# Layer 0 of a four-layer convolution kernel: two depthwise blocks on channel groups of 32 split by row and column parity, one tap of each VectorE block as a ScalarE product added by a transfer, images kept singly

## The chip, the cores and the metric

The kernel runs on one core of a Trainium2 chip. A core has a matrix engine (TensorE, "PE" in the profile, with its weight loads as "PEld"), a vector engine (VectorE, "DVE"), an engine for pointwise functions (ScalarE, "ACT"), a general engine (GpSimd, "POOL"), an engine that only issues transfers (SyncE, "SP") and 16 DMA engines that move data. The metric is the device time of one execution in microseconds. Each engine takes its instructions strictly in its own order; semaphores tie the engines to each other.

## What is computed

The input x has 32 images of 96 channels with 56 by 56 pixels, in float32. Four layers follow each other, each of the form x + f(norm(x)), where norm is a group norm over three channels. The change touches layer 0 alone. Cut to what matters, layer 0 is

```
xn = group_norm(x)
h  = einsum('nchw,oc->nohw', xn, w_exp)          # 96 -> 576 channels
h  = silu(bn1(h))
h  = depthwise 3x3 convolution(h, w_dw)          # each channel by itself, zero padding
h  = silu(bn2(h))
s  = sigmoid(w_se2 @ silu(w_se1 @ mean(h)))      # one factor per image and channel
h  = einsum('nchw,oc->nohw', h * s, w_proj)      # 576 -> 96 channels
y  = x + (bn3(h) + xn)
```

Layers 1 to 3 (a wavelet convolution, a quantised bottleneck, a 9x9 convolution) are the same before and after the change.

## The kernel before, in words

**Blocks.** The 576 channels of layer 0 stand in blocks of 128 partitions. The depthwise convolution of blocks 0, 1 and 2 is made tap by tap on 128x3136 tiles: the first tap by ScalarE (`first_tap`, L349), the other eight by VectorE as h = pad * w + h (`tap`, L354), 24 instructions an image. Block 3 ("ab") and the half block 4 ("c") go through TensorE: `quarters` (L382) multiplies a 64x64 diagonal matrix per tap with shifted windows of a padded tile, in the four 64x64 quarters of the array, nine taps accumulated in PSUM. Float32 matmuls appear twice in the trace, as two passes, so one call of `quarters` is 36 matmuls and 72 rows of the trace. There are six calls an image (four for ab, two for c).

**Steps.** All work on an image is cut into short steps, written as a letter and numbers:

- s, u, m, q, v, w, b, n: the group norm. s and q are ScalarE sums (L281), u and v small matmuls, m, w and b small VectorE work, w with a power on GpSimd (L302). n writes the normalised image xn (ScalarE, L315), of which there is one buffer.
- e: `expand`, one matmul group of w_exp (L329) and its eviction with silu by ScalarE into a padded tile (L341). `e20` is block 2, quarter 0 of the rows.
- f, t: the taps of blocks 0 to 2. z: `end_block`, the second silu in place with its sum over the pixels (L360). a, c: the depthwise calls for ab and c with their evictions (L360).
- g: the factors per channel: totals (VectorE), two sets of small matmuls (L412, L419), a sigmoid (L426, with a load of its function table), and the scaling of w_proj (L430).
- r: ScalarE prepares the residual in place (L321). p: `project` (L441 to L443), a quarter of the rows each, 20 rows of the trace. d: VectorE adds it to the image (L449). o: channel statistics for the next layer (L90), the store of the image, the fetch of a later one.

**Order.** `L0_ORDER` is one row of such steps, run once per image; a "-" behind a step means the image before, "--" the one before that, "+" the next. `run_steps` walks the row for n = -2 to 33 and issues every step for the image it names. For TensorE, VectorE and ScalarE this written order is the order on the engine (`manual_schedule`). SyncE and GpSimd get theirs from the framework, which here follows the program's order.

**PSUM.** Steps e, a, c and p share one pool of three buffers ("mm"), given out in turn: each such step waits until the one three places earlier in the row has been read out.

**Transfers.** Images come and go in pairs. `fetch` (L215) loads two images at once into one of two tiles of 2352 KB. After the second image of a pair `store_images` writes both into six scratch tensors of 16 channels (L166, six DMAs). In these tensors the four phases of 14 columns of all images lie beside each other, so the contiguous run is 112 bytes for a pair and 56 bytes for one image; the last two images are stored singly (L166 for image 30, L153 for image 31). In between, SyncE issues transfers that build filter matrices for layers 1 and 3 (`aside`, L567 and L594), a share of them at each store, until image 27. All of these stand in one queue. A fetch waits until the tile that it overwrites has been stored.

**Start.** Image 0 is normalised first; then the filter tables of layers 1 and 3 are made, on GpSimd above all, in memory that layer 0 takes over afterwards ("late" tiles: three of the five h tiles, the ab and c tiles, the second image tile). `fetch(2)` is issued when that memory is free.

The functions that the change touches, with the line numbers of the profile:

Of the kernel before, what the change touches and what calls it, by code (L numbers as in the profile page):

```python
# [21 lines left out]
HW = H * W  # L22
# [14 lines left out]
HALO = 4  # L37
MAGIC = 12582912.0
# [23 lines left out]
    e00 e01 e02 e03 z0- f0 a3- z2- c1- e10 e11 t01 t02 g0- e12 t03 e30 e40 g1- e13 t04 g2- g3-  # L62
    e31 e32 t05 e33 g4- t06 t07 s+ f1 t11 p0- u+ m+ p1- q+ t08 d0- v+ w+ p2- t12 e41 d1- p3- d2- t13
    t14 e20 e21 d3- o- b+ t15 e42 t16 e43 e22 e23 f2 a0 t17 t21 a1 n+ t22 t18 t23 t24 t25 t26 t27 r
    z1 t28 c0 a2
# [115 lines left out]
def layer0(ctx, tc, S, x, w, y0, norm1, tables, aside):  # L181
# [16 lines left out]
    DV, AB, CC = 3, 3, 4  # L198
    ND = NBLK + 1
    COL = (0, 1, 2, 3, 5)  # L200
# [8 lines left out]
    pairs = [cp.tile([C, H * NPH, 2, W4], F32, tag="xt0", name="xt0")]  # L209

    def fetch(b):

        if b < B:
            pair = pairs[b // 2 % 2]
            nc.sync.dma_start(pair, x[b // 2])  # L215
            for j in range(2):
                xs[b + j] = pair, pair[:, :, j, :]
# [3 lines left out]
    wexp = load("l0_wexp", [C, NBLK * 128])  # L221
    mid = load("l0_mid", [128, 9, ND])
    wdw = load("l0_wdw", [128, ND, 9])
    wse1 = load("l0_wse1", [128, ND, SEH])
    wse2 = load("l0_wse2", [SEH, ND * 128])
    bse1 = load("l0_bse1", [SEH, 1])
# [4 lines left out]
    for j in range(2):  # L231
        g, b_, m, v = (mid[:, 4 * j + i, :] for i in range(4))
        r = cp.tile([128, ND], F32, tag=f"r{j}", name=f"r{j}")
        nc.gpsimd.tensor_scalar(r, v, EPS_L0, None, ALU.add)
        nc.gpsimd.tensor_tensor(r, r, S.mhalf[:, :ND], ALU.pow)
        s = cp.tile([128, ND], F32, tag=f"s{j}", name=f"s{j}")
        nc.vector.tensor_tensor(s, g, r, ALU.mult)
        o = cp.tile([128, ND], F32, tag=f"o{j}", name=f"o{j}")
        nc.vector.tensor_tensor(o, m, s, ALU.mult)
        nc.vector.tensor_tensor(o, b_, o, ALU.subtract)  # L240
        sc.append(s)
        bi.append(o)
# [8 lines left out]
    diag = cp.tile([128, 2, 9, HALF], F32, tag="diag", name="diag")  # L251
    hpad = padded(cp, nc, 3, F32, "hpad") + padded(cp, nc, 1, F32, "hhalf", HH)
# [3 lines left out]
    eye2 = h2s[1].rearrange("p h w -> p (h w)")[:, :HALF]  # L256
    nc.vector.tensor_tensor(eye2, S.ident[:, :HALF], S.ident[:, HALF:], ALU.add)
    for k in (AB, CC):
        for t in range(9):
            nc.vector.tensor_scalar(diag[:, k - AB, t, :], eye2, wdw[:, COL[k], t : t + 1], None, ALU.mult)  # L260

    ims = {}

    def image(b):

        if b not in ims:
            pair, xt = xs.pop(b)
            ims[b] = {
                "b": b, "pair": pair, "xt": xt, "h2": [None] * DV, "ps": [None] * NP,
                "pad": [hpad[(DV * b + k) % 2] for k in range(DV)] + hpad[2:],  # L270
                "ss": sm.tile([128, ND], F32, tag="ss", name="ss"),
            }
        return ims[b]
# [49 lines left out]
    def expand(im, k, i):  # L323

        c = COL[k]
        rows = slice(2 * i * RT, 2 * (i + 1) * RT)
        ps = psum.tile([128, 2, 512], F32, tag="mm", name="ps")
        for j in range(2):
            nc.tensor.matmul(  # L329
                ps[:, j, :NT], wexp[:, k * 128 : k * 128 + 128],  # L330
                im["xn"][:, j, rows, :].rearrange("c h w -> c (h w)"), start=True, stop=True,
            )

        parts = [(slice(128), 2 * i * RT, slice(2 * RT))]
        if k == CC:
            lo, up = slice(64), slice(64, 128)
            parts = [(up if i // 2 else lo, i % 2 * 2 * RT, slice(2 * RT))]
            parts += [[], [(up, -1, slice(2 * RT - 1, 2 * RT))], [(lo, HH, slice(1))], []][i]
        for p, r0, rows in parts:
            n = rows.stop - (rows.start or 0)  # L340
            nc.scalar.activation(  # L341
                window(im["pad"][k][p], p.stop - (p.start or 0), 0, 0, r0, n).rearrange("p r (w j) -> p j r w", j=2),
                ps[p, :, :NT].rearrange("p j (r w) -> p j r w", w=W2)[:, :, rows],
                AF.Silu, bias=bi[0][p, c : c + 1], scale=sc[0][p, c : c + 1],
            )
# [16 lines left out]

    def end_block(im, k):
        silu2(k, im["h2"][k], im["h2"][k], im["ss"][:, k : k + 1])
# [5 lines left out]
    def quarters(k, pad, tiles):  # L370

        ps = psum.tile([128, 2, 512], F32, tag="mm", name="psd")
        for t in range(9):
            for j in range(2):
                for r in range(2):
                    c = r ^ j
                    p = slice(r * HALF, (r + 1) * HALF)
                    at = (2 * tiles[r] * RT + t // 3) * PITCH + t % 3  # L380
                    v = pad[p, at : at + 2 * RT * PITCH].rearrange("p (r w) -> p r w", w=PITCH)
                    nc.tensor.matmul(  # L382
                        ps[c * HALF : (c + 1) * HALF, j, :NT].rearrange("p (r q m) -> p r q m", q=W4, m=2),
                        diag[p, k - AB, t, :], phases(v[:, :, :W], j), start=(t == 0), stop=(t == 8),
                    )
        return ps

    def depthwise_ab(im, i):
        if i == 0:
            im["hab"] = hab  # L390
            im["pab"] = sm.tile([128, 2, NP], F32, tag="pab", name="pab")
        ps = quarters(AB, im["pad"][AB], (i, i))
        for j in range(2):
            silu2(3 + j, im["hab"][:, i, j, :], ps[:, j, :NT], im["pab"][:, j, i : i + 1])

    def depthwise_c(im, i):

        if i == 0:
            im["hc"] = hc
            im["pc"] = sm.tile([128, 2], F32, tag="pc", name="pc")  # L400
        ps = quarters(CC, im["pad"][CC], (i, i))
        silu2(5, im["hc"][:, i], ps[:, :, :NT], im["pc"][:, i : i + 1])


    def totals(im):
        nc.vector.tensor_reduce(im["ss"][:, 3:5], im["pab"], AX.X, ALU.add)
        nc.vector.tensor_tensor(im["ss"][:, 5:6], im["pc"][:, 0:1], im["pc"][:, 1:2], ALU.add)

    def squeeze(im):
        ps = psm.tile([SEH, 1], F32, tag="sm", name="pse")  # L410
        for k in range(ND):
            nc.tensor.matmul(ps, wse1[:, k, :], im["ss"][:, k : k + 1], start=(k == 0), stop=(k == ND - 1))  # L412
        im["s1g"] = sm.tile([SEH, 1], F32, tag="s1g", name="s1g")
        nc.scalar.activation(im["s1g"], ps, AF.Silu, bias=bse1, scale=1.0 / HW)
# [7 lines left out]
    def gates(im):  # L422
        gt = im["gate"] = sm.tile([128, ND + 1], F32, tag="gate", name="gate")
        nc.vector.tensor_tensor(gt[:, :ND], im["pg"], mid[:, 8, :], ALU.add)
        nc.vector.tensor_tensor(gt[:, ND:], im["pg"][:, ND - 1 : ND], mid[:, 8, ND - 1 : ND], ALU.add)
# [7 lines left out]
    def project(im, i):  # L433
# [3 lines left out]
        for j in range(2):  # L437
            out = ps[:C, j, :NT].rearrange("c (m r q) -> c r q m", m=2, q=W4)
            hab, hc = (im[n].rearrange("p i j (r q m) -> p i j r q m", q=W4, m=2) for n in ("hab", "hc"))
            for k in range(DV):  # L440
                nc.tensor.matmul(out, wg[:, k, :], phases(im["h2"][k][:, rows], j), start=(k == 0), stop=False)  # L441
            nc.tensor.matmul(out, wg[:, 3 + j, :], hab[:, i, j], start=False, stop=False)  # L442
            nc.tensor.matmul(out, wg[:, 5 + (i // 2 ^ j), :], hc[:, i % 2, j], start=False, stop=True)  # L443
# [10 lines left out]
    def store(im):  # L454
        b = im["b"]
        channel_stats(nc, sm, im["xt"], mv_all[:, b, :], "t")
        store_images(nc, y0, im)
        if b % 2:
            fetch(b + 3)
# [10 lines left out]
        "e": expand, "f": first_tap, "t": tap, "z": end_block, "a": depthwise_ab, "c": depthwise_c,  # L470
# [11 lines left out]
    hab = late.tile([128, NP, 2, NT], F32, tag="hab", name="hab")  # L482
    wg = late.tile([128, ND + 1, C], F32, tag="wg", name="wg")
    h2s.append(late.tile([128, H, W], F32, tag="h24", name="h24"))
    hc = late.tile([128, 2, 2, NT], F32, tag="hc", name="hc")
    pairs.append(late.tile([C, H * NPH, 2, W4], F32, tag="xt1", name="xt1"))
# [836 lines left out]
def layouts(a):  # L1323
# [29 lines left out]
    def columns(names, blocks):  # L1353
        return np.stack([blocks(a[n]) for n in names], axis=1)

    i0, i2 = "L0_conv_", "L2_conv_"
# [4 lines left out]
        "l0_wexp": np.concatenate([a[i0 + "w_exp"], a[i0 + "w_exp"][512:]]).T,  # L1361
        "l0_mid": columns(
            [i0 + n for n in ("g1", "b1", "m1", "v1", "g2", "b2", "m2", "v2", "b_se2")], quartered
        ),
        "l0_wdw": quartered(a[i0 + "w_dw"].reshape(MID, 9)),
        "l0_wse1": quartered(a[i0 + "w_se1"].T),
        "l0_wse2": quartered(a[i0 + "w_se2"]).transpose(2, 1, 0).reshape(SEH, (NBLK + 1) * 128),
        "l0_bse1": a[i0 + "b_se1"].reshape(SEH, 1),
        "l0_wproj": apart(quartered(a[i0 + "w_proj"].T)),
# [44 lines left out]
```

## Time and profile before

| What | Value |
|---|---|
| Three timed runs, us | 6365.32, 6370.07, 6379.44; median 6370.07 |
| Profiled execution, span, us | 6375.2 (what lies around the span is not given) |
| Layer 0, first expand to last VectorE add | 28 to 3233 us |
| VectorE busy, 100 to 1600 us (layer 0) | 1415.85 of 1500 |
| TensorE busy, the same stretch | 1465.64 |
| ScalarE busy, the same stretch | 988.69 |
| DMA share, the same stretch | 0.23 |
| First fetch, issue to first use | 0.72 to 14.07 us |
| Fetch behind the tables, issued | 96.65 us |
| First tap of image 0, of image 31 | 41.4 us, 3091.3 us |
| End of the last tap in layer 0 | 3193 us |
| Start of the norm that closes layer 0 | 3236.8 us |

The page gives busy time by engine, by slice of the span and by group of instructions; a group names the line, the engine, the operation, its output and inputs, the number of instructions, their busy time and mean duration, and the idle time ahead of them with what ended it. Concurrent matmuls count once in "busy" and each for itself in "mean". One image of layer 0 takes about 99 us, so a sum per image and engine is the natural unit.

### The profile page before, as it was taken

The page shows a single profiled execution, that of the slowest core. Times are in us where ns is not written, and L with a number is a line of the kernel's source. Part 1 is how long each engine was busy: PE and PEld are TensorE (multiplying, and loading weights), DVE is VectorE, ACT ScalarE, POOL GpSimd, SP SyncE. Part 2 cuts the span into 40 slices and gives each one's busy share as a digit, 9 for nine tenths or more (in the row PEclk, how much of TensorE's full clock was granted, in tenths as well). Part 3 has the DMA queues.
Part 4 walks back from the last instruction along what each step waited for, and adds up shares of the span by engine and source line. Part 5 has one row for each costly group of instructions (what it writes and reads, how often), then busy time and mean ns, then how long its engine had stood idle before and what let it go on. Part 6 is the DMA issues. An engine that isn't in the chain of part 4 may idle for free.

```text
span 6375.2 us, 115759 instructions
## 1 busy us (share of the span) xinstructions
PE 6012.5 (94%) x49064; PEld 3561.4 (56%) x49064; DVE 5173.6 (81%) x5533; ACT 4051.7 (64%) x5716; POOL 236.1 (4%) x157
## 2 busy tenths in 40 slices
PE   6999999999999999999969999989999999999699
PEld 3444444444444444444445666667777777777344
DVE  8999999999999999999947666667777776776577
ACT  6667676676666766667535655567767676776355
POOL 5000000000000000000000000000000000000000
PEclk8999999999999999999979999999999999999899
DMA  3112222122221222212465866568787786863788
GB/s 96 17 38 57 50 45 35 42 55 54 41 36 36 51 54 43 42 26 37 24 90 145 152 147 146 127 29 54 42 53 41 51 44 46 48 46 27 183 249 245
DMA packets 1305764, 452.95 MB, mean 71 GB/s; under 512 B 1123150, under 2 KB 1301062, under 8 KB 1303326
## 3 DMA queue, kind: packets, MB, share of 16 engines
q1 hardware_dynamic: 1305246, 445.54, 47.3%
q8 instruction: 386, 6.32, 0.5%
q14 instruction: 132, 1.08, 0.1%
HBM read 284.44 MB, written 214.08 MB: 78 GB/s over the span
## 4 chain that ended last, share of the span: by engine, by line
PE 72%; ACT 14%; DMA 6%; DVE 4%; SPq 2%; issue 1%; POOL 1%; ACTq 0%; DVEq 0%; POOLq 0%
PE psd L382 18%; PE psd L1066 11%; PE ps L329 11%; PE pc L782 6%; PE ps L1047 6%; PE psj L441 5%; ACT junk L281 4%; PE psj L1103 3%; DVE h L354 2%; DMA raw<-tdiff 2%; ACT hi L1019 2%; DMA X<-y 2%; ACT hpad L341 2%; PE psj L442 2%; PE pc L766 2%; ACT a L1037 2%
## 5 line engine op out<-in xcount | busy, mean ns | idle before, releaser
L354 DVE SCALAR_TENSOR_TENSOR h<-hpad,l_wdw,h 128x3136 f32<-128x3136 f32 x768 | 2662.4, 3481 | 37.3 <-ACT h L349 23.5
L1066 PE MATMUL psd<-apad,diag 64*64 64x392 bf16 x20736 | 927.1, 331 | 96.3 <-ACT a L1037 51.6
L329 PE MATMUL ps<-xn,l_wexp 96*128 96x392 f32 x2560 | 893.1, 500 | 6.4 <-ACT xn L315 4.4
L1066 PEld LDWEIGHTS <-diag 64*64 64x64 bf16 x20736 | 691.3, 107 | 328.0 <-issue 151.1
L382 PE MATMUL psd<-hpad,diag 64*64 64x392 f32 x9216 | 831.1, 511 | 0.0
L341 ACT ACTIVATE hpad<-ps,o,s 128x784 f32<-128x784 f32 x512 | 545.7, 1081 | 302.5 <-PE ps L329 299.2
L329 PEld LDWEIGHTS ps<-xn,l_wexp 96*128 96x128 f32 x2560 | 478.6, 191 | 374.9 <-issue 36.5
L612 ACT COPY T<-raw 32x112 f32<-32x112 f32 (+2 forms) x1440 | 462.8, 384 | 312.2 <-DMA raw<-tdiff 229.3
L1037 ACT ACTIVATE u<-ps,o,s 128x784 int16<-128x784 f32 x576 | 536.7, 1003 | 159.8 <-PE ps L1047 140.9
L441 PE MATMUL psj<-h,wg 128*96 128x392 f32 x1536 | 603.8, 529 | 17.0 <-DVE wg L430 8.0
L1037 ACT ACTIVATE a<-psd,o,s 128x784 int16<-128x784 f32 x448 | 424.1, 998 | 305.8 <-PE psd L1066 305.7
L382 PEld LDWEIGHTS psd<-hpad,diag 64*64 64x64 f32 x9216 | 347.1, 131 | 467.6 <-issue 433.0
L1047 PE MATMUL ps<-hi,l_w1q 96*128 96x392 f32 x1280 | 461.5, 361 | 9.2 <-ACT hi L1019 9.2
L1220 PE MATMUL pc<-x,T 128*112 128x416 f32 (+1 forms) x1152 | 416.9, 524 | 52.0 <-DMA raw<-tdiff 48.1
L782 PE MATMUL pc<-x,T 128*112 128x416 f32 (+1 forms) x1152 | 445.1, 522 | 0.0
L1047 PE MATMUL ps<-lo,l_w1q 96*128 96x392 f32 x1280 | 437.2, 342 | 0.0
L382 PE MATMUL psd<-hhalf,diag 64*64 64x392 f32 x4608 | 417.6, 510 | 0.0
L441 PEld LDWEIGHTS psj<-h,wg 128*96 128x96 f32 x1536 | 247.0, 166 | 285.8 <-issue 250.7
L341 ACT ACTIVATE hhalf<-ps,o,s 64x56 f32<-64x56 f32 (+1 forms) x192 | 163.6, 852 | 342.3 <-PE ps L329 340.5
L1220 PEld LDWEIGHTS pc<-x,T 128*112 128x112 f32 x1152 | 203.7, 178 | 264.7 <-issue 236.1
L360 ACT ACTIVATE hab<-psd,o,s 128x392 f32<-128x392 f32 x256 | 170.9, 672 | 248.6 <-PE psd L382 248.6
L382 PEld LDWEIGHTS psd<-hhalf,diag 64*64 64x64 f32 x4608 | 182.7, 132 | 223.0 <-issue 223.0
(209 smaller groups left out, 7673.6 us busy)
## 6 DMA issues: line engine op xcount, KB each, us to landing
X<-y SPq DMA_DIRECT2D x192, 392.0 KB
y<-xt SPq DMA_DIRECT2D x180, 392.0 KB
xt<-in_x_dram SPq DMA_DIRECT2D x16, 2352.0 KB
y<-y SPq DMA_DIRECT2D x96, 392.0 KB
xt<-y SPq DMA_DIRECT2D x96, 392.0 KB
out_dram<-y SPq DMA_DIRECT2D x96, 392.0 KB
twav<-zwav SPq DMA_DIRECT2D x768, 36.8 KB
raw<-twav SPq DMA_DIRECT2D x96, 168.0 KB
```

Source lines behind the costliest of these rows:

```text
L281: nc.scalar.activation(junk, im["xt"][:, i * 2 * RT * NPH : (i + 1) * 2 * RT * NPH], func, bias=bias, accum_out=im[name][:, i : i + 1])
L329: nc.tensor.matmul(ps[:, j, :NT], wexp[:, k * 128 : k * 128 + 128], im["xn"][:, j, rows, :].rearrange("c h w -> c (h w)"), start=True, sto ...
L341: nc.scalar.activation(window(im["pad"][k][p], p.stop - (p.start or 0), 0, 0, r0, n).rearrange("p r (w j) -> p j r w", j=2), ps[p, :, :NT] ...
L354: nc.vector.scalar_tensor_tensor(h2, window(im["pad"][k], 128, t // 3 - 1, t % 3 - 1, 0, H), wdw[:, k, t : t + 1], h2, ALU.mult, ALU.add,)
L382: nc.tensor.matmul(ps[c * HALF : (c + 1) * HALF, j, :NT].rearrange("p (r q m) -> p r q m", q=W4, m=2), diag[p, k - AB, t, :], phases(v[:, ...
L441: nc.tensor.matmul(out, wg[:, k, :], phases(im["h2"][k][:, rows], j), start=(k == 0), stop=False)
L612: nc.scalar.copy(to.rearrange("x t (p s) -> x t p s", p=NPH), v[:, k])
L782: nc.tensor.matmul(ps[:PH, to], st["T"][j][:, h, k, :], st["x"][:, j, h, of], start=False, stop=(n == NK - 1))
L1037: nc.scalar.activation(out, ps, AF.Identity, bias=o[:, c : c + 1], scale=s[:, c : c + 1])
L1047: nc.tensor.matmul(ps[:, j, :NT], w1[:, k * 128 : k * 128 + 128], im[part][:, r0 : r0 + RT, :].rearrange("c h w -> c (h w)"), start=(part ...
L1066: nc.tensor.matmul(ps[q, j, :NT].rearrange("p (r w) -> p r w", w=W), diag[p, k, t, :], v, start=(t == 0), stop=(t == 8))
L1220: nc.tensor.matmul(ps[:, :, to], st["T"][:, h, k, :], st["x"][:, h, :, of], start=(n == 0), stop=(n == NK - 1))
```

## The change

Blocks 3 and 4 leave the padded tiles. Their 192 channels form six groups of 32. A group's expanded image is written as a "plane" of 128 partitions: four copies of the 32 channels, one for each parity of row and column, each of 28 by 28 pixels. `expand_phases` makes one plane by eight matmuls of 96x32 and one eviction. `filtered` makes the depthwise convolution for four groups (or parts) at once: a 128x32 matrix sums up to four taps in one matmul; taps that cross to a neighbouring row of planes use the lower or the upper 64 partitions. A call is 32 matmuls, six calls an image as before.

Of each VectorE block tap 8 is made by ScalarE into a tile `tmp` (there is one) and added to h by a DMA that GpSimd issues (`product`, step x). VectorE keeps seven taps.

Images are held singly in three tiles; each is stored and fetched by itself. The row of steps is another, with the image's work spread over three rows.

```
-    e00 e01 e02 e03 z0- f0 a3- z2- c1- e10 e11 t01 t02 g0- e12 t03 e30 e40 g1- e13 t04 g2- g3-
-    e31 e32 t05 e33 g4- t06 t07 s+ f1 t11 p0- u+ m+ p1- q+ t08 d0- v+ w+ p2- t12 e41 d1- p3- d2- t13
-    t14 e20 e21 d3- o- b+ t15 e42 t16 e43 e22 e23 f2 a0 t17 t21 a1 n+ t22 t18 t23 t24 t25 t26 t27 r
-    z1 t28 c0 a2
+    t05- g0-- f1- z2-- e30- t06- g1-- g2-- g3-- g4-- t07- x08- e20- e23- s t11- p3-- p1-- d3-- r- u
+    e21- t12- t13- e22- m d1-- t14- q p0-- t15- v p2-- z0- t16- w t17- x18- f2- b n d0-- d2-- a0-
+    a3- a2- e00 t21- t22- e01 t23- e02 t24- t25- e03 z1- t26- t27- a1- x28- f0 c0- c1- e10 e12 e13
+    e33 e32 o-- e11 e31 e40 t01 t02 t03 t04 e41
...
+    images = [cp.tile([C, H * NPH, W4], F32, tag="xt0", name="xt0")]
     def fetch(b):
         if b < B:
-            pair = pairs[b // 2 % 2]
-            nc.sync.dma_start(pair, x[b // 2])
+            xs[b] = images[b % 3]
+            nc.sync.dma_start(xs[b], x[b])
...
+    def expand_phases(im, g):
+        ps = psum.tile([128, 2, 512], F32, tag="mm", name="pse")
+        c = DV * 128 + g * GC
+        for half in range(2):
+            for f in range(4):
+                r0 = half * HH + f // 2
+                nc.tensor.matmul(
+                    ps[f * GC : (f + 1) * GC, half, :NT].rearrange("p (r w) -> p r w", w=W2), wexp[:, c : c + GC],
+                    im["xn"][:, f % 2, r0 : r0 + HH - 1 : 2, :], start=True, stop=True,
+                )
+        nc.scalar.activation(
+            planes[g].rearrange("p (j r) w -> p j (r w)", j=2), ps[:, :, :NT],
+            AF.Silu, bias=bi[0][:, DV + g : DV + g + 1], scale=sc[0][:, DV + g : DV + g + 1],
+        )
...
+    def product(im, k, t):
+        nc.scalar.activation(tmp, window(im["pad"][k], 128, t // 3 - 1, t % 3 - 1, 0, H), AF.Copy, scale=wdw[:, k, t : t + 1])
+        nc.gpsimd.dma_start(im["h2"][k], tmp, accum_op=ALU.add, max_dma_last_dim=2 * HW)
...
-    def quarters(k, pad, tiles):
+    def filtered(parts, p):
         ps = psum.tile([128, 2, 512], F32, tag="mm", name="psd")
...
+        rounds = [[(r, 2 * r + p, every, 0, 0)] for r in range(2)] + [[(r, 4 + 2 * r + p, every, 0, q)] for r in range(2)]
+        rounds += [[(0, n, low, -1, dq), (1, n, top, 1, dq)] for n, dq in ((8 + p, 0), (10 + p, q))]
...
+        for i, products in enumerate(rounds):
+            for at, (g, half) in enumerate(parts):
+                for r, m, rows, dm, dq in products:
...
+                    nc.tensor.matmul(
+                        ps[at * GC : (at + 1) * GC, r, :NT].rearrange("p (r w) -> p r w", w=W2)[
+                            :, r0 - half * n : r1 - half * n, q0:q1],
+                        filt[rows, g * NM + m, :], planes[g][rows, r0 + dm : r1 + dm, q0 + dq : q1 + dq],
+                        start=(i < 2), stop=(i == len(rounds) - 1),
+                    )
...
     def project(im, i):
+            for k, h in enumerate(im["h2"] + [im["hab"]]):
+                nc.tensor.matmul(out, wg[:, k, :], phases(h[:, rows], j), start=(k == 0), stop=False)
+            half = slice(i % 2 * 2 * RT, (i % 2 + 1) * 2 * RT)
+            nc.tensor.matmul(out, wg[:, 4 + i // 2, :], phases(im["hc"][:, half], j), start=False, stop=True)
...
     def store(im):
         b = im["b"]
         channel_stats(nc, sm, im["xt"], mv_all[:, b, :], "t")
-        store_images(nc, y0, im)
-        if b % 2:
-            fetch(b + 3)
+        if b < B - 1:
+            for to, of in groups(im["xt"], y0, lambda y: y[:, :, b, :], store=True):
+                nc.sync.dma_start(to, of)
+        fetch(b + 3)
...
+    images.append(late.tile([C, H * NPH, W4], F32, tag="xt1", name="xt1"))
+    tmp = late.tile([128, H, W], F32, tag="tmp", name="tmp")
+    hc = late.tile([128, HH, W], F32, tag="hc", name="hc")
+    images.append(late.tile([C, H * NPH, W4], F32, tag="xt2", name="xt2"))
+    fetch(1)
+    fetch(2)
```

The evictions of a and c keep their number of six PSUM buffers, with one ScalarE instruction of 128x784 for each where ab had two of 128x392. Weights and factors are laid out anew on the host to fit.

## Prediction

> **What bounds the kernel now.** I read the page's totals, then one stretch of layer 0, then its groups, waits and order in time. The page's totals mix four layers, so the stretch comes first:
>
> ```profile
> 1508.00:1707.00 199.00, 194.66 (x1256) 94.05 (x1252) 187.27 (x107) 131.25 (x153) 7.26 (x2) 0.98 0.23 44
> ```
>
> Two images: TensorE is busy 194.66 of 199 us, VectorE 187.27, ScalarE 131.25, at a granted clock of 0.98. Two engines bound together; relieving one alone would gain a few us. Groups of 300 to 2900 us (mean ns of one behind the comma):
>
> ```profile
> L354 DVE SCALAR_TENSOR_TENSOR h<-hpad,l_wdw,h 128x3136 f32<-128x3136 f32 x632 | 2191.2, 3481 | 30.8 <-ACT h L349 19.5
> L329 PE MATMUL ps<-xn,l_wexp 96*128 96x392 f32 x2096 | 726.6, 497 | 0.0
> L382 PE MATMUL psd<-hpad,diag 64*64 64x392 f32 x7636 | 689.0, 511 | 0.0
> ...
> L349 ACT ACTIVATE h<-hpad,l_wdw 128x3136 f32<-128x3136 f32 x79 | 229.5, 2905 | 0.8
> ```
>
> A tap costs VectorE 3.48 us, a first tap ScalarE 2.9 us. An expand matmul is worth 726.6/2096 = 0.347 us. The waits of the same stretch:
>
> ```profile
> POOL rstd L302 <- DVE ve L300: 2477.4, 26, 95.6
> ...
> DVE xt L449 <- PE psj L443: 96.1, 26, 3.7
> ```
>
> The first gives the period: 2477.4 plus the 94.4 busy of that group, over 26, is 98.9 us an image. The second is VectorE's largest idle time, 3.7 us an image; with three smaller ones (1.6, from VectorE's own order in time) it idles 5.3 and works 93.6. TensorE in order of time:
>
> ```profile
> 1506.20 6.56 PE L382 MATMUL psd<-hpad,diag 64*64 64x392 f32 x72
> 1512.59 6.51 PE L382 MATMUL psd<-hhalf,diag 64*64 64x392 f32 x72
> 1519.03 6.85 PE L329 MATMUL ps<-xn,l_wexp 96*128 96x392 f32 x20
> ```
>
> A depthwise call starts 6.4 us after the one before: 18 groups of four rows, 0.355 us a group, so four 64x64 quarters do run at once. The SyncE queue:
>
> ```profile
> 1666.60 33.40 SPq L166 DMA_DIRECT2D y<-xt  x6
> 1700.04 7.01 SPq L567 DMA_DIRECT2D twav<-zwav  x1
> 1710.89 0.34 SPq L215 DMA_DIRECT2D xt<-in_x_dram  x1
> ```
>
> A pair's store occupies SyncE for 33.4 us, and its fetch is issued 44 us after the store began. The single store of image 30 shows what 56-byte runs cost:
>
> ```profile
> 3147.25 30.16 SPq L166 DMA_DIRECT2D y<-xt  x6
> ```
>
> So a single image takes nearly as long as a pair: same number of runs, half the bytes.
>
> **The change, step by step, per image.**
>
> *VectorE.* Three taps go: 3 x 3.50 (start to start) = 10.5, leaving 93.6 - 10.5 = 83.1 us. Nothing is added.
>
> *TensorE before:* 80 x 0.347 = 27.7 expand, 6 x 6.42 = 38.5 depthwise, 4 x 6.8 = 27.2 project, 2.5 small: 95.9 of 98.9. *After:* blocks 0 to 2 keep 48 rows, 16.6. Six planes are 48 matmuls, 96 rows, four column tiles at once: 24 x 0.355 = 8.5. A filtered call has 64 rows: 32 of 128x32 in 8 groups of four and 32 of 64x32 in 4 groups of eight, 12 x 0.355 = 4.3; six give 25.6. Project 27.2, small 2.2. Sum 80.1. The trace has no 32-column tile. Low end: the quarters' rate as above, since each tile streams the same 392 columns. High end: two streams per 64 partitions at a time, all that the quarters show; then 24 groups a call (51.1) and 48 for the planes (17.0), sum 114. Between: 64x32 tiles only four at a time, 16 groups a call, sum 88.6. I take 80.1, as the quarters are the nearest row.
>
> The Trainium skill (TensorE: Matmul & The Clock Gate, Measured speedup vs the span model) gives 2.38 times for three column tiles, 0.79 each. No row here has column tiles of 32. By it four tiles give 3.17 times, a group 4 x 0.34/3.17 = 0.43 us, the sum 87 and the period 95 with the waits below: an estimate that takes away two thirds of the gain.
>
> *ScalarE.* 65.6 now. Three products of 2.9 add 8.7 (nearest row L349). Planes are 6 instructions of 1.08 in place of 8 of 1.08 and 2 of 0.4, -3.0. Ab needs 4 of 1.2 instead of 8 of 0.87, -2.1. Sum 69 of some 88: covered, but ScalarE stands in order, so waits count.
>
> *Added waits.* Each z step waits for its accumulating transfer. Such a transfer isn't in the trace. It moves 1.6 MB; a fetch of 2.41 MB took 11.7 us, so a copy is 7.8, and as an addition must read its destination too, twice that, 15.7, is the high end undisturbed. Beside a store the 16 engines are half busy (share 50.7% for a pair), so the far end is 31. Issue by GpSimd: its power took 0.58 us early and 3.3 later:
>
> ```profile
> 24.38 0.58 POOL L302 TENSOR_TENSOR rstd<-ve,mhalf 96x1 f32<-96x1 f32 x1 [4.88 <-DVE ve L300]
> ...
> 168.12 3.34 POOL L302 TENSOR_TENSOR rstd<-ve,mhalf 96x1 f32<-96x1 f32 x1 [76.86 <-DVE ve L300]
> ```
>
> that is, up to a tap longer once taps run back to back. I take L = 15 in all. The Trainium skill (SBUF — State Buffer, Who interferes with whom) says a VectorE instruction with two SBUF inputs blocks GpSimd instructions that read SBUF, not ones that only write; by it the power waits and issuing doesn't. Nothing else here rests on that.
>
> From VectorE's order I place the slack: between tap 27's end and the gates of the same image VectorE has 26 us of other work (o, t01 to t04, t05, t06); z2 (3.2), squeeze, excite and their activation (3.7) come out of it, so a transfer of up to 19 us is hidden. x08 and x18 have about 20 too. Past that the period is 66 + L. Behind a late z on ScalarE stand evictions, hence TensorE.
>
> *What then is late.* The row's tightest ring runs through TensorE: last plane evicted (1.1), f1 (2.9), z2 (3.2), squeeze to scaled weights (4.8 with the table load), then project. In these 12 us TensorE has only 6 of work: 6 idle. Some 20 changes of tile shape at about 0.1 us (6.42 per call against 18 x 0.35) are 2. So the period is 80.1 + 6 + 2 = **88.3 us**, above VectorE's 83.1.
>
> *SyncE's queue* per image: store and landing 39, fetch 0.3, filter transfers 40.5 (81 for two images in its order of time), 80 in all, where a pair shares 44 today. The fetch is due 57 us after the last add; store plus a half-size fetch (6) and landing take 47. Both fit below 88 by 8 to 10 us; the accumulating transfers eat into that.
>
> *Ends.* Image 1 is now fetched behind the tables (issue at 96.7 as today's second fetch), so its m comes at about 109, which sets the first full row's start to 85. Then 31 rows, of which the first lacks adds and statistics (-11), 66 in the last row to tap 27, 15 for the transfer, and 44 from there to the closing norm (3193.0 to 3236.8 today): 199 + 31 P. With P = 88.3: 2936, against 3237, **-301**. The sum stands on the profile's span, 6375 - 301 = 6074; the median of the runs is 5 below the span: 6069, and I say **6070 us**.
>
> **Rivals.**
>
> *A: transfers instead of engines.* Late accumulations, or a store slowed by them, set the period. For: 56-byte runs at full DMA share (118.3% in the store of image 30 against 50.7% for a pair), a queue already at 80 of 88, 4.8 MB more to move. Against: the store is limited by its issue (30 us for 21504 runs), and large packets would take turns with it. At L = 31 the period is 97, the sum 6375 - 31 - 5 = 6339. If two transfers of 7.8 to 15.7 stop the store wholly, the queue gives 96 to 111; past 98 it is slower, up to 6770.
>
> *B, the slower side: 32-column tiles don't stream four at a time.* Place: planes and filtered calls, 96 groups an image. Each 0.01 us a group adds 0.96 us; it decides at a group of 0.46 us (46 for the rest, 8 waits, 98 period). Two at a time gives P = 122, 3981, 7114 us. For: no row shows more than two streams over one set of partitions. Against: the quarters run four tiles at full rate.
>
> *C: it doesn't do what it says:* the PSUM turn order, with p0 waiting for d1 and a3 for d0, keeps a period of 97 to 99 though every engine has less to do: about 6370. Against: by VectorE's order d1 ends at 25 us of the row and d0 at 41, close to where TensorE arrives anyway.
>
> **Numbers.** Forecast 0.52 (period 85.5 to 90.5: 5983 to 6140); A 0.24 (6140 to 6480, of it 0.18 faster, 0.02 same, 0.04 slower); B 0.16, slower; C 0.08 (0.02 faster, 0.02 same, 0.04 slower). Faster by over 0.2% (what a measurement of this kernel can tell from none) 0.72, same 0.04, slower 0.24. The range runs from a period of 85.5, near VectorE's floor, to A's reach, 5983 to 6480: it leaves out most of B and the tail of A, about 0.18.
>
> **What would show it.** VectorE with 21 taps an image and idle under 6; a filtered call's 64 rows starting 4.3 us apart; z waiting under 1 us for a transfer; s not waiting for a fetch; layer 0 closing near 2936. Wrong: calls of 6 us and more (B), s or z behind DMA (A), a period of 98 with idle everywhere (C).

## The result and the profile after

The changed kernel takes 6405.6 us (median of 4 runs, 6399.5 to 6425.3) against 6367.7 for the kernel before: a ratio of 1.006, 95% interval 1.0042 to 1.0078. The forecast was 6070 us and "faster"; it is slower by 0.6%. The profiled execution of the changed kernel has a span of 6397.7 us (its own time 6399.5). GpSimd's closing power of layer 0's norm, the row that follows the closing norm's first step by 2.7 us, says where the difference lies. First before, then after:

```profile
3239.47 5.43 POOL L110 TENSOR_TENSOR row<-nve,mhalf 96x32 f32<-96x32 f32 x1
```

```profile
3269.10 5.45 POOL L111 TENSOR_TENSOR row<-nve,mhalf 96x32 f32<-96x32 f32 x1
```

Layer 0 ends 29.6 us later, where 301 earlier was forecast. Behind it the two kernels differ little: layer 1's and layer 3's norm transfers lie 2686 us apart before and 2688 after, and from the closing power to the end of the span after needs 7 us less. The same stretch of layer 0 that the prediction began with, now after (time, then busy time of TensorE, its weight loads, VectorE, ScalarE and GpSimd, then granted clock, DMA share, GB/s):

```profile
1508.00:1707.00 199.00, 166.39 (x1248) 75.30 (x1247) 157.55 (x95) 136.89 (x133) 14.55 (x8) 0.88 0.93 88
```

Both engines that bounded the kernel have lost work: TensorE from 194.66 to 166.39 us, VectorE from 187.27 to 157.55. Neither is near the stretch's 199 us, and the DMA share went from 0.23 to 0.93; a slow store lies in this stretch, and over 100 to 1600 us the share is 0.65. The arithmetic runs as forecast. TensorE in order of time, three filtered calls each:

```profile
1522.40 12.61 PE L402 MATMUL psd<-plane,filt 128*32 128x392 f32 x192
...
1540.40 12.60 PE L402 MATMUL psd<-plane,filt 128*32 128x392 f32 x192
```

12.6/3 is 4.2 us a call. What ends ScalarE's, and behind it TensorE's, idle time is new (waits of 300 to 2900 us, that is 26 images; total, times, longest):

```profile
ACT junk L286 <- DMA xt<-in_x_dram: 375.7, 24, 31.2
...
PEld pn L291 <- ACT junk L286: 236.6, 19, 25.3
...
ACT h L374 <- DMA h<-tmp: 7.8, 4, 2.6
```

The first step of an image's statistics waits for the image itself, 14.4 us an image. The accumulated tap (last line) is waited for four times in all. SyncE itself waits for transfers; for an engine it waits under 3 us in all 26 images:

```profile
SPq L216 <- DMA y<-xt: 108.6, 26, 8.6
SPq L596 <- DMA xt<-in_x_dram: 88.6, 26, 6.1
...
SPq L484 <- ACT hpad L339: 2.4, 6, 0.6
```

Its queue shows why the image is late. Two images of after; each line is a start, how long SyncE issued, and how many transfers:

```profile
1537.47 50.26 SPq L484 DMA_DIRECT2D y<-xt  x5
1587.78 6.00 SPq L596 DMA_DIRECT2D twav<-zwav  x1
1602.66 0.33 SPq L216 DMA_DIRECT2D xt<-in_x_dram  x1
1603.04 13.00 SPq L596 DMA_DIRECT2D twav<-zwav  x11
...
1635.24 16.20 SPq L596 DMA_DIRECT2D tdiff<-zdiff  x16
1651.57 34.96 SPq L484 DMA_DIRECT2D y<-xt  x6
1686.57 4.54 SPq L596 DMA_DIRECT2D twav<-zwav  x1
1695.12 0.34 SPq L216 DMA_DIRECT2D xt<-in_x_dram  x1
1695.51 9.29 SPq L596 DMA_DIRECT2D twav<-zwav  x11
...
1729.30 16.21 SPq L596 DMA_DIRECT2D tdiff<-zdiff  x16
1745.65 25.10 SPq L484 DMA_DIRECT2D y<-xt  x4
```

From one store's begin (1651.57) to the next (1745.65) are 94 us: 35 for the store, 5 for the filter transfer right behind it, 4 until the store has landed, 0.3 for the fetch, 50 for the other filter transfers. 16 filter transfers, beside which an accumulating transfer runs, take 16.2 us to issue; in the kernel without accumulating transfers (below) they take 10.0, about 0.6 us each. The image above it (number 13) has a store that is issued for over 50 us and landed only after 64, so its fetch leaves 66 us after the store began. That fetch brings image 16 into the same tile, and GpSimd's power, one an image, shows the delay (images 14 to 16):

```profile
1417.22 3.65 POOL L307 TENSOR_TENSOR rstd<-ve,mhalf 96x1 f32<-96x1 f32 x1 [32.44 <-DVE ve L305]
...
1516.03 3.67 POOL L307 TENSOR_TENSOR rstd<-ve,mhalf 96x1 f32<-96x1 f32 x1 [32.43 <-DVE ve L305]
...
1631.24 3.65 POOL L307 TENSOR_TENSOR rstd<-ve,mhalf 96x1 f32<-96x1 f32 x1 [41.27 <-DVE ve L305]
```

The starts are 98.8 and 115.2 us apart. Over layer 0, seven periods are 110 to 117 (mean 114.4), each three images behind a slow store, and the other 24 have a mean of 94.3. Above 88.7, the engines' own period as found below, the first make 180 us and the second 134: 314 of the 330 us between forecast and result.

Single stores are late for images 2, 6, 9, 13, 18, 22, 25 and 29 only, a pattern that repeats after 16 (behind image 29 nothing is fetched, hence seven long periods). An image's run is 56 bytes at 56 times its number. In these eight, and no others, the run crosses a multiple of 128 bytes and leaves on both sides a piece that isn't a multiple of 32 (16 + 40, 48 + 8, 8 + 48, 40 + 16); images 4, 11, 20 and 27 cross too, with a piece of 32 beside one of 24, and aren't late. By this trace's packets a 56-byte run took 10 ns in the mean in most stores and 39 to 74 in the late ones. Long packets alone don't make a store late, though: before's single store of image 30, which crosses no such multiple, had 35 ns a run and landed after 40 us.

### The profile page after: what moved, and what is told of

Read it like the earlier page. It is cut to its first block, busy times and chain, and to the rows that moved or that the text cites. A ratio compares the mean times of both kernels' runs of the same rounds, so it can differ in the third digit from the quotient of the medians.

```text
span 6397.7 us, 116536 instructions
## 1 busy us (share of the span) xinstructions
PE 5636.5 (88%) x49448; PEld 3309.8 (52%) x49448; DVE 4848.8 (76%) x5422; ACT 4212.7 (66%) x5428; POOL 351.5 (5%) x247
## 4 chain that ended last, share of the span: by engine, by line
PE 59%; SPq 16%; DMA 13%; ACT 7%; issue 2%; DVE 2%; POOL 1%; ACTq 0%; POOLq 0%; DVEq 0%
PE psd L1095 11%; SPq L484 10%; PE ps L1076 6%; PE pc L1249 6%; PE pc L811 6%; PE psd L402 6%; DMA y<-xt 6%; PE psj L466 5%; PE ps L335 5%; SPq L596 5%; DMA xt<-in_x_dram 3%; PE psj L1132 3%; ACT hi L1048 2%; DMA twav<-zwav 2%; PE pc L795 2%
## 5 line engine op out<-in xcount | busy, mean ns | idle before, releaser
L368 DVE SCALAR_TENSOR_TENSOR h<-hpad,l_wdw,h 128x3136 f32<-128x3136 f32 x672 | 2334.5, 3478 | 20.4 <-ACT h L363 5.5
L402 PE MATMUL psd<-plane,filt 128*32 128x392 f32 (+5 forms) x12288 | 811.0, 486 | 4.7 <-issue 4.7
L335 PE MATMUL ps<-xn,l_wboth 96*128 96x392 f32 x1536 | 671.5, 593 | 10.1 <-issue 5.7
L402 PEld LDWEIGHTS psd<-plane,filt 128*32 128x32 f32 (+1 forms) x12288 | 285.3, 108 | 523.1 <-issue 469.6
L339 ACT ACTIVATE hpad<-ps,o,s 128x784 f32<-128x784 f32 x384 | 415.9, 1093 | 164.0 <-PE ps L335 145.8
L335 PEld LDWEIGHTS ps<-xn,l_wboth 96*128 96x128 f32 x1536 | 335.5, 228 | 296.5 <-issue 128.1
L286 ACT ACTIVATE junk<-xt 96x784 bf16<-96x784 f32 x128 | 109.6, 856 | 393.3 <-DMA xt<-in_x_dram 390.3
L374 ACT ACTIVATE h<-h,o,s 128x3136 f32<-128x3136 f32 x96 | 287.0, 2990 | 24.9 <-DMA h<-tmp 24.9
L379 ACT ACTIVATE tmp<-hpad,l_wdw 128x3136 f32<-128x3136 f32 x96 | 278.4, 2900 | 35.7 <-DMA zdiff<-zt 35.7
L363 ACT ACTIVATE h<-hpad,l_wdw 128x3136 f32<-128x3136 f32 x96 | 278.8, 2904 | 14.8 <-PE psj L466 14.7
## 6 DMA issues: line engine op xcount, KB each, us to landing
h<-tmp POOLq DMA_DIRECT2D x96, 1568.0 KB, 14.4
```

The lines of the kernel that those rows point to most:

```text
L335: nc.tensor.matmul(ps[:, j, :NT], wexp[:, k * 128 : k * 128 + 128], im["xn"][:, j, rows, :].rearrange("c h w -> c (h w)"), start=True, sto ...
L339: nc.scalar.activation(window(im["pad"][k], 128, 0, 0, 2 * i * RT, 2 * RT).rearrange("p r (w j) -> p j r w", j=2), ps[:, :, :NT].rearrange ...
L368: nc.vector.scalar_tensor_tensor(h2, window(im["pad"][k], 128, t // 3 - 1, t % 3 - 1, 0, H), wdw[:, k, t : t + 1], h2, ALU.mult, ALU.add,)
L402: nc.tensor.matmul(ps[at * GC : (at + 1) * GC, r, :NT].rearrange("p (r w) -> p r w", w=W2)[:, r0 - half * n : r1 - half * n, q0:q1], filt[ ...
```

## Experiments

Three theories were put: T1, SyncE's queue (single stores and filter transfers) brings the image late; T2, the accumulating transfers slow what else is moved; T3, the turns in PSUM or the granted clock hold the period. A kernel's ratio is to before, run beside it on the same chip; the experiments used three chips. "Closing power" is the GpSimd row shown above.

**Filters of 8 channels only.** Both lists stop at channel 8, and layers 1 and 3 read channel c % 8.

```diff
-[lambda c=c: wavelet_matrices(nc, z1, z2, z3, t1, t2, t3, c) for c in range(C)]
-+ [lambda c=c: matrix_rows(nc, td[c], zd[c], 1) for c in range(C)])
+[lambda c=c: wavelet_matrices(nc, z1, z2, z3, t1, t2, t3, c) for c in range(8)]
++ [lambda c=c: matrix_rows(nc, td[c], zd[c], 1) for c in range(8)])
```

> After, with the filters of layers 1 and 3 laid out for channels 0 to 7 only, which all channels then use; the filters of the other 88 channels, and 11 of 12 of the filter transfers inside layer 0, are left out. T1 (the SyncE queue sets the period: 35 store, 5 ring, 4 landing, 50 filter transfers, and 22 more for a slow store): the queue falls to 44 us an image, 66 with a slow store, the engines' ring decides, a period of 88 us, layer 0's closing norm near 2940, the total near 6080. T2 (the accumulating transfers slow the stores and what else is moved; the filters matter little): the slow stores stay late, a period of 94 to 97, closing norm 3110 to 3200. T3 (the order of PSUM or the TensorE clock keeps the period): 97 to 99 still, closing norm 3220 to 3270.

Measured: 6349.6 us, ratio 0.9939 (0.9919 to 0.996); closing power at 3192.7. T1's total was missed by 270 us, and the closing norm, 3190, lies in T2's range; yet T2 wanted 94 to 97 throughout, and the periods fall in two clear classes: 87 to 93 for regular images, 115 to 120 after a late store.

```profile
1449.95 3.67 POOL L307 TENSOR_TENSOR rstd<-ve,mhalf 96x1 f32<-96x1 f32 x1 [25.34 <-DVE ve L305]
...
1566.95 3.65 POOL L307 TENSOR_TENSOR rstd<-ve,mhalf 96x1 f32<-96x1 f32 x1 [46.75 <-DVE ve L305]
...
1660.03 3.66 POOL L307 TENSOR_TENSOR rstd<-ve,mhalf 96x1 f32<-96x1 f32 x1 [26.81 <-DVE ve L305]
```

SyncE's queue of this kernel around them:

```profile
1456.81 65.23 SPq L484 DMA_DIRECT2D y<-xt  x5
1542.95 0.34 SPq L216 DMA_DIRECT2D xt<-in_x_dram  x1
1574.55 43.50 SPq L484 DMA_DIRECT2D y<-xt  x6
1625.74 0.32 SPq L216 DMA_DIRECT2D xt<-in_x_dram  x1
```

SyncE now has 31 us without anything to issue ahead of a regular store, so the sum of the queue no longer counts. The late store does: its fetch leaves 87 us after the store began (the first of its six transfers is off the top), where it is due 57 after the last add. So T1 had two parts that I had run together: the queue's sum holds the regular images at 94 to 99, and a late landing holds up the fetch by itself. In this run the last filter transfer of layer 0 is issued at 1157 us, so none stands between the stores shown.

**No tap 8.** x08, x18 and x28 are struck from the order, so tap 8 of blocks 0 to 2 is left out.

> After, with tap 8 of blocks 0 to 2 left out: no product on ScalarE, no accumulating transfer; VectorE still does 21 taps. T1: filter transfers are issued at 0.58 us throughout, so the queue falls from 94 to 80 us in a regular image, and the slow stores remain (60 us, the same images): 102 there, a period of 90 to 92 in the mean, closing norm 3000 to 3060, total 6140 to 6200. T2: no store over 45 us is left and the period is 88 throughout: closing norm near 2940. T3: 97 to 99 still, closing norm 3220 to 3270.

Measured: 6235.0, ratio 0.976 (0.9734 to 0.9787); closing power at 3084.6. Regular periods 88.4 to 93, after late stores 102 to 107; the same eight images are late (landing after 65 to 74 us, on this chip; 80 to 86 with the accumulating transfers in the kernel above). The closing norm, 3082, is above both theories' (3000 to 3060, 2940). The accumulating transfers have a share in both delays: beside them the late stores are about 12 us longer, and the slower issue puts the regular image's queue over the engines' time; without them SyncE issues the filter transfers behind a fetch in 39 us instead of 50. They aren't what makes a store late.

**Before with single images.** Three tiles of one image in place of two pairs.

```diff
-pairs = [cp.tile([C, H * NPH, 2, W4], F32, tag="xt0", name="xt0")]
+images = [cp.tile([C, H * NPH, W4], F32, tag=f"xt{i}", name=f"xt{i}") for i in range(2)]
...
-        store_images(nc, y0, im)
-        if b % 2:
-            fetch(b + 3)
+        if b < B - 1:
+            for to, of in groups(im["xt"], y0, lambda y: y[:, :, b, :], store=True):
+                nc.sync.dma_start(to, of)
+        fetch(b + 3)
```

> Before, with three tiles of one image each in place of two of a pair: each image fetched and stored singly, the arithmetic as before. No accumulating transfer is in it. T1: slow stores (59 to 66 us) in images 2, 6, 9, 13 and the like of the next sixteen; the queue needs 80 us in a regular image and 102 in a slow one, just about before's period of 98.9, so the total is 6370 to 6430. T2: all stores take about 40 us, the total stays within 0.2% of before. T3 says nothing of it.

Measured: 6493.1, ratio 1.0162 (1.0139 to 1.0186), above T1's 6430; closing power at 3325.7. Regular periods stay at 97.3 to 100, and after images 2, 6, 9, 13 and so on they are 110 to 116. A late store without any accumulating transfer:

```profile
1504.09 52.80 SPq L457 DMA_DIRECT2D y<-xt  x6
1556.94 8.31 SPq L566 DMA_DIRECT2D twav<-zwav  x1
1576.48 0.33 SPq L215 DMA_DIRECT2D xt<-in_x_dram  x1
1576.86 9.55 SPq L566 DMA_DIRECT2D twav<-zwav  x11
1586.45 1.20 SPq L593 DMA_DIRECT2D twav<-zwav  x2
```

So single images by themselves cost the old arithmetic 86 us of layer 0. I had expected a period of 99 to cover the late store; the fetch, again, is due earlier than that.

**Layer 3's filters on GpSimd's queue.** matrix_rows gets a queue, and the calls for td pass nc.gpsimd.

> After, with the filter transfers of layer 3 (4 of the 18 that a channel has) issued on GpSimd's queue. T1: SyncE issues 14 transfers less per image, 12 us of its 94, a period of 88 to 91 in the mean, closing norm 2940 to 3040, total 6080 to 6200, unless GpSimd's own work (the power, the accumulating transfers) gets late behind the new issues. T2: the same bytes move beside the accumulations, so no more than 2 us of the period go: total 6340 to 6410. T3: no change.

Measured: 6428.4, ratio 1.0074 (1.0056 to 1.0091), above what T1 and T2 gave. From image 16 on, where an image has 42 transfers left on SyncE, regular periods are 88.7 to 92.1, as T1 says. The late stores land after 78 to 88 us, about as on the same chip in the first experiment (80 to 86), and the long periods behind them, 116 to 130, take it back.

**Slots turned by one.** Image b is stored in slot b + 1.

```diff
-lambda y: y[:, :, b, :], store=True
+lambda y: y[:, :, (b + 1) % (B - 1), :], store=True
```

> After, with image b's single store put into the slot of image b+1 (the 31st into slot 0), so the images of layer 0's result are in another order, which the later layers don't undo. T1a (a 56-byte run that crosses a 128-byte line with a piece on both sides that isn't a multiple of 32 bytes is slow): the slow stores (60 us and more) are now those of images 1, 5, 8, 12, 17, 21, 24 and 28; time unchanged, closing norm 3250 to 3285. T1b (something in the order of the work, such as the filter transfers or the tiles' rotation, makes them slow): they stay at images 2, 6, 9, 13, 18, 22, 25, 29.

Measured, one run: 6601.7, with late stores at images 1, 5, 8, 12, 17, 21, 24 and 28. They follow the slot: T1a. The time unchanged that it forecast was missed: the closing power is at 3446.2, and these stores landed after 77 to 84 us where after's needed 60 to 69. So it was run again on another chip:

> The kernel with single stores turned by one slot once more (images in another order in layer 0's result). There its slow stores took 77 to 84 us where after's took 60 to 69, and the total was 6602. If that belongs to the kernel: again 6570 to 6630. If it was that execution or that chip: 6400 to 6450.

Measured: 6418.8, ratio 1.008 (1.0045 to 1.0115), the same eight stores late, at 64 to 70 us, closing power 29 us behind after's. On the two chips the same kernel's late stores differ by up to a quarter, while before differs by 0.3%. With one run on the first chip, chip and execution aren't separated. The totals of the kernels with 56-byte stores are therefore compared only on one chip, with before beside them.

**Halves beside each other.** Rows p and p + 112 of an image lie side by side, in the image tile ([C, 112, 2, 14]) and in layer 0's result, so a run is 28 numbers, 112 bytes. This halves the number of runs, and it also takes the late places away: an image's run now starts at 112 times its number, and wherever it crosses a multiple of 128 bytes, one of its pieces is a multiple of 32 (16 + 96, 32 + 80, 48 + 64 and the reverse).

```diff
-images = [cp.tile([C, H * NPH, W4], F32, tag="xt0", name="xt0")]
+images = [cp.tile([C, PH, 2, W4], F32, tag="xt0", name="xt0")]
...
-for to, of in groups(im["xt"], y0, lambda y: y[:, :, b, :], store=True):
+for to, of in groups(im["xt"].rearrange("c x h q -> c x (h q)"), y0,
+                     lambda y: y[:, :, b].rearrange("g x h q -> g x (h q)"), store=True):
...
+for h, v in enumerate((rows[0, :, :HALO], rows[1, :, -HALO:])):
+    for p in range(NPH):
+        nc.sync.dma_start(X[PH + p * HALO : PH + (p + 1) * HALO, :, h], v[p, :, :, 1 - h])
```

> After, with the rows of the upper and the lower half of an image beside each other in layer 0's image tiles and in its result, so a single store has 10752 runs of 112 bytes instead of 21504 of 56; normalising takes 8 instructions instead of 4, layer 1 loads its border rows in 8 transfers instead of 2. All else, accumulating and filter transfers too, is as in after. T1: a store is issued in 16 to 18 us and lands by 24, none is slow, the queue needs 72 to 76 us an image, and the period is the 88.8 of the regular images without filters: closing norm 2960 to 3000, total 6090 to 6170. T2 (accumulating transfers are what costs): period 94 to 97, total 6290 to 6390.

Measured: 6240.8, ratio 0.9765 (0.9746 to 0.9784). All stores land after 25 to 30 us, and every period from the third on is 88.7 to 88.8. The closing power is at 2947.6, so layer 0 is 322 us shorter than after's. The total is 70 us over the expectation, because what follows gives 140 us back: layer 1's and layer 3's norm transfers lie 2829 us apart in place of 2688. SyncE in layer 1, one channel:

```profile
3503.46 0.36 SPq L737 DMA_DIRECT2D X<-y  x1
3503.86 5.25 SPq L741 DMA_DIRECT2D X<-y  x8
3509.16 0.47 SPq L684 DMA_DIRECT2D nr<-norm  x1
```

Eight border transfers take 5.25 us to issue; after's two take 1.3. VectorE waits for the matrices queued behind them (3450 to 4000 us; after shows no such wait there):

```profile
DVE x L759 <- DMA raw<-twav: 118.2, 30, 14.9
```

**The same with 8 channels' filters.**

> The kernel with 112-byte runs, and the filters of layers 1 and 3 laid out for channels 0 to 7 only (the other 88 channels' filters left out). T1: the queue was no longer the bound, so the closing norm comes within 15 us of that of the 112-byte runs alone. If filter transfers still cost: 30 us and more earlier. If 88.8 us isn't the engines' own ring: the period falls below 88.

Measured, one run: closing power at 2945.7, 2 us from the kernel before it; periods 88.7. The filter transfers are free once the store is short, and 88.7 us is the engines' own ring, the chain of waits among them that closes once an image.

**Before's arithmetic with halves beside each other.**

> Before's arithmetic with single images, stored in 112-byte runs as in the run with halves beside each other. T1: no slow store, the queue well below the engines' 97.3 us an image; closing norm 3215 to 3245, total within 0.5% of before (6340 to 6400). So what single images cost is the runs, and what the new arithmetic gains is the difference to the after kernel with 112-byte runs, 250 to 290 us. T2 says the same of this kernel, and a difference of under 100 us.

Measured: 6535.9, ratio 1.0231 (1.0214 to 1.0249), closing power at 3240.7, periods 99.0: layer 0 as expected, the total missed by layer 1's 150 us. In layer 0 the new arithmetic is 293 us ahead of this kernel, just above the 250 to 290 given.

**Two border transfers.** One transfer per half, over all 16 rows.

```diff
-    for p in range(NPH):
-        nc.sync.dma_start(X[PH + p * HALO : PH + (p + 1) * HALO, :, h], v[p, :, :, 1 - h])
+    nc.sync.dma_start(X[PH:, :, h], v[:, :, :, 1 - h])
```

> The after kernel with 112-byte runs, but layer 1's border rows loaded in 2 transfers a channel (512 runs of 56 bytes each) instead of 8. Layer 0 as in the run with 8: a period of 88.7 us. Layer 1 gave 150 us back there, as SyncE issued 8 border transfers of 0.65 us a channel where after issues 2. If the number of issues is what costs: SyncE needs 4 us less a channel, layer 1 takes as long as in after within 30 us, total 6080 to 6130. If the runs of 56 bytes cost, or VectorE's reading of the new order: 6190 and more.

Measured: 6118.8 us (5 runs, 6106.5 to 6133.7), ratio 0.9572 (0.9551 to 0.9592): 4.3% below before, within what was expected. The two border transfers take 2.8 us and more (the first about 0.65), and the norm transfers lie 2728 us apart, 40 above after's where 30 was given. This keeps the whole change, computes all of the reference, and differs from after only in how the rows lie and move. The stretch of the prediction once more, in this kernel:

```profile
1508.00:1707.00 199.00, 186.44 (x1333) 85.13 (x1335) 186.43 (x112) 157.41 (x157) 18.19 (x9) 0.95 0.51 99
```

Its periods, closing power and queue:

```profile
1437.10 3.65 POOL L313 TENSOR_TENSOR rstd<-ve,mhalf 96x1 f32<-96x1 f32 x1 [25.32 <-DVE ve L311]
...
1525.84 3.66 POOL L313 TENSOR_TENSOR rstd<-ve,mhalf 96x1 f32<-96x1 f32 x1 [25.32 <-DVE ve L311]
...
1614.59 3.66 POOL L313 TENSOR_TENSOR rstd<-ve,mhalf 96x1 f32<-96x1 f32 x1 [25.33 <-DVE ve L311]
...
2944.03 5.45 POOL L111 TENSOR_TENSOR row<-nve,mhalf 96x32 f32<-96x32 f32 x1
```

```profile
1532.09 21.18 SPq L494 DMA_DIRECT2D y<-xt  x6
1553.32 4.55 SPq L606 DMA_DIRECT2D twav<-zwav  x1
1561.27 0.33 SPq L222 DMA_DIRECT2D xt<-in_x_dram  x1
1561.65 14.16 SPq L606 DMA_DIRECT2D twav<-zwav  x11
```

And what the queue itself waits for, 300 to 2900 us:

```profile
SPq L494 <- DVE xt L482: 341.2, 29, 64.4
```

88.74 and 88.75 us apart; the fetch leaves 29 us after the store began; and the store now waits for VectorE's last add, 341.2/29 = 11.8 us an image: the queue has slack where after's had none. No wait of ScalarE for an image is left between 300 and 2900 us, where after has 375.7 us. Per period TensorE is busy 186.44 x 88.75/199 = 83.1 us, VectorE 83.1, ScalarE 70.2. TensorE's squeeze waits for the last block's silu (step z2), 5.6 us an image:

```profile
PEld pse L446 <- ACT h L382: 162.3, 29, 5.6
```

**Before's arithmetic with both.**

> Before's arithmetic with single images in 112-byte runs, and layer 1's border rows in 2 transfers a channel. Period 99.0 us, total 6370 to 6420. So with the transfers out of the way in both, the change of the arithmetic alone is worth what the prediction worked out, some 10 us an image and 290 us in all.

Measured: 6426.0, ratio 1.0056 (1.004 to 1.0071), 6 us above the range; periods 99.0, closing power at 3236.9. It ran beside the kernel above: with the same rows and transfers in both, the new arithmetic is worth 6426.0 - 6118.8 = 307 us, 293 of them in layer 0.

**Two border transfers, no tap 8.** Tap 8 of blocks 0 to 2 is left out again.

> The kernel with 112-byte runs and 2 border transfers, and tap 8 of blocks 0 to 2 left out (no product, no accumulating transfer). If the accumulating transfers are hidden once the store is short: a period of 88.7 again, the closing power within 10 us of 2944, total 6100 to 6130. If they still cost: a period of 86 or less.

Measured: 6098.5 (2 runs), ratio 0.9576 (0.9548 to 0.9604), periods 88.7, closing power at 2936.7, 7 us earlier. The accumulating transfers are hidden. What is left of them and of their products lies at the end of the layer: from the last image's power to the closing power are 165 us, where the kernel with tap 8 has 176.

## Why the prediction was wrong

- *VectorE, 93.6 to 83.1 us.* Right: 83.1 in the kernel whose queue has slack.
- *TensorE, 80.1 and some 2 of seams; a filtered call 4.3.* Right: 83.1 and 4.2. Four 128x32 tiles and eight 64x32 tiles ran at once, so rival B falls. My estimate of 0.43 us a group, from the 2.38 times for three column tiles that the Trainium skill gives (TensorE: Matmul & The Clock Gate, Measured speedup vs the span model), was too long: 12 groups in 4.2 us are 0.35, and the measurement decides.
- *ScalarE 69.* Right: 70.2, with four more instructions of normalising in that kernel.
- *Accumulating transfer, L = 15, hidden.* Right: in after the median from issue to landing is 14.8 us in layer 0, waited for 7.8 us in 26 images, and leaving it out of the last kernel moves no period. It was not harmless, though: see the queue below. Issuing it costs GpSimd 1.2 us with taps running back to back, where its power takes 3.65: so far the rule quoted from the Trainium skill (SBUF — State Buffer, Who interferes with whom) agrees with the trace.
- *Period 88.3, closing norm 2936, -301.* Right as a ring of the engines: 88.7, and with the queue out of the way the closing norm is at 2944.0 - 2.7 = 2941. The ring is the one named: TensorE waits 5.6 us an image for z2, where 6 was given. Wrong for the kernel that was changed.
- *What failed:* the queue, "80 in all", of which the prediction says "Both fit below 88 by 8 to 10 us; the accumulating transfers eat into that." Two terms were mis-sized. The filter transfers were put at 40.5 and take 55 us, 5 of them for the one right behind the store and some 10 more than given for the rest, slowed while an accumulation runs, so the regular queue is 94, not 80; the regular periods' excess over 88.7 made 134 of the 330 us missed. And 39 for store and landing was read from one single store, image 30's; eight of the 31 single stores take 60 to 69, and the seven long periods made 180. Nothing in before's trace shows such a slot: its pair stores land after 40 to 43 us throughout. But I had written down that the transfers eat into a margin of 8 to 10 us, and then gave the engines' period as the forecast without a size for what they eat.
- *Rival A, 0.24.* It is what happened, by its place (the queue, s waiting for the fetch) and by its sum: 96 to 111 was given, a mean near 99 came. Its reason was half of it: the accumulations slowed the filters' issue more than the store. The late slots were in no rival. Its sum for L = 31 kept 15 us for the last image's transfer; with 31 there too, 6339 would be 6355.
- *Rival C.* The period of 97 to 99 came, but not from PSUM's turns: with the rows side by side and the store shorter for it, the same order of steps runs at 88.7. The granted clock of 0.88 went with the idle time: 0.95 where that is gone.

Left open: how much of the shorter store's gain comes from fewer runs and how much from the places, as no run changed one without the other; and why just these four places in 128 bytes are late. The trace shows longer packets and no reason, and other ways to divide a run weren't tried. The Trainium skill (DMA: Bandwidth & Descriptors, Specifications) says that a transfer under 512 bytes is done by read-modify-write; all runs here are under 512 bytes, and most are not late, so that rule alone doesn't tell these slots from the others.

## What to carry to other kernels

When a change makes the engines faster, add up each queue against the new period, not the old one, with its slowest member in it: a queue at nine tenths of the period is no cover. A fetch that waits for a store is due at its own time, and one late store in four holds an image up by most of its delay, whatever the queue's mean. Look at a store's runs, their number and where they lie, and not only at its bytes: two rows side by side halved the number of runs and left none in a late place, and with the border rows loaded in two transfers the same change of the arithmetic went from 0.6% slower to 4.3% faster.

## What the hardware showed that was not expected

- A store of 56-byte runs takes longer at certain places: 21504 runs land after 40 to 44 us in most slots and after 60 to 69 in four of sixteen (with the slots turned by one, 64 to 70 on one chip and 77 to 84 on another). No slot was late with 112-byte runs, none of which leaves such pieces.
- An accumulating transfer of 1568 KB lands after 12.2 us in the median (two border transfers) to 14.8 (after), and while it runs SyncE's issue of small filter transfers goes from 0.6 to about 1.0 us each. GpSimd issues it in 1.2 us, also while VectorE's taps run back to back (after, 300 to 2900 us):

```profile
L380 POOL DMA_DIRECT2D h<-tmp x77 | 92.7, 1204 | 1532.9 <-PE ps L335 646.5 <-PE psd L402 504.3 <-DVE h L368 375.6
```

- Issue goes by runs in large transfers: SyncE was busy some 30 us with a store of 21504 runs and 15 with one of 10752, in six transfers each and with no accumulation beside them. A border transfer of 128 runs was issued in 0.66 us, and of two with 512 runs the first in 0.65 too.
